# Splitting the token stage of batches 0 and 1: residual and second normalization moved into the next attention stage, with a new work order

## The chip, the core and the metric

The kernel runs on one core of a Trainium2 chip. A core has a matrix engine (PE, TensorE), a vector engine (DVE, VectorE), an activation engine (ACT, ScalarE), a general engine (POOL, GpSimd) and queues that issue DMAs (mostly SP's, some POOL's and ACT's). Each engine works through its own list of instructions in the order in which the program wrote them, and waits on semaphores for what it needs. The metric is the device time of one execution in microseconds (us); lower is better.

## The reference, cut to what matters

The input `x` is four images of 64 x 64 positions with 256 channels, float32. Two layers follow each other, and the batches do not depend on each other.

Layer 0 is self-attention over the 4096 positions of an image, with a residual:

```
f, g, v = xt @ Wf + bf, xt @ Wg + bg, xt @ Wh + bh
beta = softmax(einsum('bqd,bkd->bqk', g, f));  o = einsum('bqk,bkd->bqd', beta, v) @ Wo + bo
x = x + o
```

Layer 1 is a triangle attention over the 64 x 64 grid, and then a token block with two layer normalizations:

```
scores = einsum('bilhd,bljhd->biljh', q, k) / sqrt(d_k);  att = softmax(scores, axis=2)
out = einsum('biljh,bilhd,bljhd->bijhd', att, v1, v2)
h = layer_norm(x_in + out @ Wo, ln_agg_g, ln_agg_b)              # first norm
z = relu(h @ W1 + b1) @ W2 + b2 + h                              # MLP and residual
result = layer_norm(z, ln_out_g, ln_out_b)                       # second norm
```

The change concerns the last two lines of the token block (the residual `+ h` and the second norm) for batches 0 and 1, and the order in which the triangle's work of batches 1 and 2 is written out.

## The kernel before, in words

**Stages.** For each batch `b` in turn the kernel does layer 0 (`layer0`, 64 groups) and then the triangle of layer 1 (32 steps). The token block of batch `b` is not done in its own stage. It runs inside the triangle stage of batch `b + 1` (`next_layer1`), so that PE has token matmuls to do while DVE and POOL make the triangle's products. Batch 3 has no later triangle, and its tokens are done alone at the end. So the triangle stage of batch 1 carries the tokens of batch 0, that of batch 2 those of batch 1, and that of batch 3 those of batch 2 (there `own` is true).

**An attention group** (`score`, `values`): PE makes four score matmuls, ACT takes their exponential into `e` (two buffers), PE multiplies it with the values (`o`, L571), and DVE adds it to `esum` (L578). Every eight groups a query block is closed on DVE: the partial sums (L581 to L588), a reciprocal (L600), the product `oT` (L602) and two reductions (L610). In the next group PE multiplies `oT` with the output weights (L623), DVE adds bias and residual (L624), and the six groups after it begin with a projection of that result (L638). One thing more hangs on these groups in the attention stages of batches 2 and 3: `rest.recall` brings back the tokens of batch `b - 2`, 16 tiles of 256 tokens, one every three groups, and `rest.finish` scales them by the last gain and bias on POOL (L1248, L1249) and stores them.

**A triangle step** makes eight products of 128 x 2048 (L999): five or six on DVE (`R`, three buffers), three or two on POOL (`Rp`, two buffers). PE accumulates each product with eight short matmuls (L1009), ACT copies the result out (L1019), and SP stores it.

**A token tile** of 256 tokens goes through these words: `h0 h1` the output projection plus residual in PSUM (`hp`, L1081 and L1086), `sa` its mean and variance (L1097, L1098), `rr` and `pp` the inverse root (ACT, then seven tiny instructions on POOL), `fa` the first norm (`h`, L1158), `ht` its transpose on PE (L1181), `hT` and `hU` two scaled copies of the transpose (L1186; `hU` makes the one for the residual, with gain and both biases), `m0 m1 r0 r1` the hidden layer (L1214, L1223), `z0 z1` the second matmuls (L1234) followed by four transposes that add the residual in PSUM (`zp<-ident,hT`, L1240), `so` the sums of the second norm on ACT (L1112, L1116), `fo` its affine step (L1158), and `fi`, which for batches 0 and 1 stores the normalized tile to DRAM (`put_off`).

**The order** of all of this is a text, `ORDER`: 70 words, repeated once per period, 20 periods. A period holds two triangle steps and one token tile. `A13/1` is "step 2i + 1, accumulate product 3, one period late"; `/2` is two periods late. The words of one engine run in the order of the text. The scores of the later pairs (`sp`, L897) are in 11 of the periods. POOL also issues the DMAs that load the next batch's factors (`spread`) during steps 24 to 29.

Of the kernel before, what the change touches and what calls it, by code (L numbers as in the profile page):

```python
# [10 lines left out]
F32 = mybir.dt.float32  # L11
# [4 lines left out]
ALU = mybir.AluOpType  # L16
AX = mybir.AxisListType

P = 128
C = 256  # L20
# [9 lines left out]
NP = T // 256  # L30
# [10 lines left out]


ORDER = """
    r0/1 A10/2 A11/2 m1/1 R14/2 R05/1 S1/1 R15/2 T10/2 sp/1 A14/2 A16/2 r1/1 e0/1 e1/1 A15/2 A05/1 T11/2 R04/1
    A04/1 z0/1 W1/1 R03/1 V1/1 fi/2 S0 z1/1 t1/1 so/1 R06/1 R00/1 c1/1 sa A03/1 R07/1 R02/1 A06/1 A02/1 A00/1
    rr/1 pp/1 W0 R01/1 A07/1 A01/1 fo/1 fa T01/1 R12/1 t0 T00/1 R17/1 h1/-1 sf/1 R13/1 h0/-1 f0/1 ht f1/1 R16/1
# [20 lines left out]
def attention_then_triangle_kernel(  # L67
# [6 lines left out]
    nc = tc.nc  # L74
    NB = x.shape[0]
# [5 lines left out]
    work = ctx.enter_context(tc.tile_pool(name="work", bufs=2))  # L81
# [29 lines left out]
    back_t = ctile([P, 4], "back")  # L111
# [50 lines left out]
    lag_bc = brow(lag, C, "lag_bc")  # L162
# [327 lines left out]
    def layer0(b, F, safe, rest, ahead):  # L490
# [238 lines left out]
        for g in range(8 * NQB):  # L729
            qb, k = divmod(g, 8)  # L730
            if b == 0 and not safe:
                for load in later[3 * g : 3 * g + 3]:
                    load()
                if g == 6:
                    fold_bias()
                if g == 20:
                    add_b2()
            if safe and k == 0 and qb + 1 < NQB:
                mx, todo = pieces(qb + 1)
                for qc, t in todo:  # L740
                    max_piece(qc, t, mx)
                row[qb + 1] = max_row(mx)
            values(g, g + 1 < 8 * NQB)

            if qb > 0 and not (qb == last and k >= 6 + late):
                for part in parts[k]:
                    part(qb - 1)
            if late and g % 2 == 0 and 0 <= g // 2 - 2 < ahead.n:
                ahead.bring(g // 2 - 2)
            if late and g % 2 == 1 and 0 <= g // 2 - 3 < ahead.n:  # L750
                ahead.turn(g // 2 - 3)
            if b > 1 and g % 3 == 0 and g < 3 * NP:
                rest.recall(NP * (b - 2) + g // 3)
            if b > 1 and g % 3 == 2 and g < 3 * NP:
                rest.finish(NP * (b - 2) + g // 3)
            if qb == last and k == 3:
                L.fetch_v1(0)
                L.fetch_v1(1)
            if qb == last and k == 5:
                if b > 0:  # L760
                    rest.load(NP * (b - 1))
                L.fetch_qk(0, True)
# [49 lines left out]
        if old:  # L812
            rest.turn(t0)
            rest.load(t0 + 1)
            rest.normed(t0)
            rest.carried(t0)
        if not late:
            values1(1)
        score(2)
# [216 lines left out]
    class Tokens:  # L1036
        def __init__(self):
            self.ios = []
            self.A, self.htp = {}, {}
            self.h, self.hT, self.hT2, self.hid, self.z, self.zp, self.hps = {}, {}, {}, {}, {}, {}, {}  # L1040
            self.mv = self.rs = None
            self.raw = {}


        def put_off(self, tt):
            b, t = divmod(tt, NP)
            if t == 0:
                self.raw[b] = dram.tile([NP, P, 2, C], F32, tag="raw", name="raw")
            nc.sync.dma_start(out=self.raw[b][t], in_=self.z.pop(tt))

        def recall(self, tt):
            b, t = divmod(tt, NP)
            self.z[tt] = work.tile([P, 2, C], F32, tag="s4", name="z")
            nc.sync.dma_start(out=self.z[tt], in_=self.raw[b][t])

        def load(self, tt, far=False):
            b, t = divmod(tt, NP)
# [332 lines left out]
    def words_of(order):  # L1390
        for w in order:
            w, late = (w.split("/") + ["0"])[:2]
            yield w, int(late)
# [58 lines left out]
    def next_layer1(b, L, rest, ahead, F):  # L1452
        own = b == NB - 1
        t0 = NP * (b - 1)


        n2, n1, n0 = NP, NP + own, NP + 2 * own
        stored, held = set(), []
        mv, rs, rn, mps = {}, {}, {}, {}

        def fetched(step):
            if F is not None and 24 <= step < 31:
                ahead.fetch(F, b + 1, step)


        def load(q, far=False):
            if q < NP or 24 + (q - NP) // 2 in stored:
                rest.load(t0 + q, far)
            else:
                held.append((q, far))  # L1470

        def was_stored(step):
            stored.add(step)
            if own and step == 26:
                held.extend((NP + q, True) for q in (2, 3, 4))
            todo, held[:] = list(held), []
            for q, far in todo:
                load(q, far)

        def moments(q):  # L1480
            if q not in mv:
                mv[q] = small.tile([P, 4, 2], F32, tag="mv", name="mv")
            rest.mv = mv[q]

        def of_piece(word, q):
            tt = t0 + q
            first, second = 1 <= q < n1, 0 <= q < n2
            if word in ("h0", "h1"):
                if 2 <= q < n0:
                    n = int(word[1])  # L1490
                    rest.heads(tt, n, new=q not in mps)
                    mps.setdefault(q, {})["h", n] = True
                    if len(mps[q]) == 2 and q + 1 < n0:
                        load(q + 1)
            elif word == "sa" and first:
                moments(q - 1)
                rest.stats(rest.hps[t0 + q], 0)
            elif word == "so" and second:
                moments(q)
                z = rest.z[t0 + q] = work.tile([P, 2, C], F32, tag="s4", name="z")  # L1500
                rest.sums_of(rest.zp[t0 + q], z, rest.mv, 2)
            elif word == "rr" and second:
                moments(q)
                rest.roots(0 if q + 1 < n1 else 2, 4)
                rs[q] = rest.rs
            elif word == "pp" and second:
                moments(q)
                rest.rs = rs.pop(q)
                rest.polish(0 if q + 1 < n1 else 2, 4, nc.gpsimd, back=back_t)
                rn[q] = rest.rn  # L1510
            elif word == "fa" and first:
                rest.rn = rn[q - 1]
                rest.affine_a(tt)
            elif word == "fo" and second:
                rest.rn = rn[q]
                rest.affine_o(tt)
            elif word == "ht" and first:
                rest.turn(tt)
            elif word == "hT" and first:
                rest.normed(tt)  # L1520
            elif word == "hU" and first:
                rest.carried(tt)
            elif word in ("m0", "m1") and first:
                n = int(word[1])
                mps[q][n] = [rest.hidden(tt, fc) for fc in (2 * n, 2 * n + 1)]
            elif word in ("r0", "r1") and first:
                n = int(word[1])
                for fc, mp in zip((2 * n, 2 * n + 1), mps[q][n]):
                    rest.rectify(tt, fc, mp)
            elif word in ("z0", "z1") and second:  # L1530
                n = int(word[1])
                rest.outputs(tt, n, new=tt not in rest.zp)
                mps.setdefault(q, {})["z", n] = True
            elif word == "fi" and second:
                (rest.finish if own else rest.put_off)(tt)

        def spread(step):
            if F is not None:
                ahead.spread(F, b + 1, step)

        step_word, scores, take_scores = step_words(L, fetched, was_stored, spread)
        mps[1] = {}
        for period in range(NP + 4):
            for word, late in words_of(ORDER):
                i = period - late
                if i == 0 and word in ("A05", "A04"):
                    for m in (4, 5) if word == "A04" else ():
                        step_word("A", 0, m)
                elif word[0] in "RATSWVtc":
                    step_word(word[0], 2 * i + int(word[1]), int(word[-1]))  # L1550
                elif word in ("sp", "sf"):
                    if (i == 0) == (word == "sf"):
                        scores(i)
                elif word in ("e0", "e1", "f0", "f1"):
                    if (i == 0) == (word[0] == "f"):
                        take_scores(i, int(word[1]))
                else:
                    of_piece(word, i)
        assert not held
        if F is not None:  # L1560
            ahead.fetch(F, b + 1, NSTEP)
# [68 lines left out]
```

## Time and profile before

| | |
|---|---|
| median of 3 runs | 3651.67 us (3650.98 to 3653.79) |
| profiled execution, its own time | 3654.27 us |
| span of that execution, first to last instruction | 3652.5 us |
| busy in the span: PE, DVE, ACT, POOL | 97%, 75%, 53%, 49% |

The stages can be read off the timeline. The two that carry the changed words are the triangle stages of batch 1 (1303 to 1744 us) and of batch 2 (2175 to 2617 us). The two that receive the moved work are the attention stages of batches 2 and 3, which begin where those end and last about 396 us each up to the first instructions of the next triangle stage. A time of one instruction in the profile is longer than the distance to the next one on the same engine where they overlap, so the working below takes distances between starts where it can.

### The profile page before, as it was taken

The page shows a single profiled execution, that of the slowest core. Times are in us where ns is not written, and L with a number is a line of the kernel's source. Part 1 is how long each engine was busy: PE and PEld are TensorE (multiplying, and loading weights), DVE is VectorE, ACT ScalarE, POOL GpSimd, SP SyncE. Part 2 cuts the span into 40 slices and gives each one's busy share as a digit, 9 for nine tenths or more (in the row PEclk, how much of TensorE's full clock was granted, in tenths as well). Part 3 has the DMA queues.
Part 4 walks back from the last instruction along what each step waited for, and adds up shares of the span by engine and source line. Part 5 has one row for each costly group of instructions (what it writes and reads, how often), then busy time and mean ns, then how long its engine had stood idle before and what let it go on. Part 6 is the DMA issues. An engine that isn't in the chain of part 4 may idle for free.

```text
span 3652.5 us, 58549 instructions
## 1 busy us (share of the span) xinstructions
PE 3544.0 (97%) x22410; PEld 1909.6 (52%) x22410; DVE 2739.5 (75%) x2326; ACT 1934.8 (53%) x4209; POOL 1805.7 (49%) x918
## 2 busy tenths in 40 slices
PE   9999899988999999999999999999999999999998
PEld 6555444434555555554455555554455555555477
DVE  4777599996555479999565549999755556999976
ACT  3444455544444367666444457676544436777654
POOL 5000199994000068889311028889722106999910
PEclk9999999999999999999999999999999999999999
DMA  9544555465111343425422153333522225341221
GB/s 174 140 130 121 137 150 143 118 135 126 52 49 52 97 116 95 94 51 104 101 80 79 58 144 92 78 89 66 129 73 78 75 83 137 91 96 47 68 69 52
DMA packets 487987, 353.38 MB, mean 97 GB/s; under 512 B 302673, under 2 KB 433489, under 8 KB 478865
## 3 DMA queue, kind: packets, MB, share of 16 engines
q1 hardware_dynamic: 438656, 322.58, 33.1%
q0 software_dynamic: 36160, 19.94, 5.1%
q10 hardware_dynamic: 12880, 7.01, 0.7%
q8 instruction: 179, 2.93, 0.3%
q14 instruction: 112, 0.91, 0.1%
HBM read 197.34 MB, written 152.04 MB: 96 GB/s over the span
## 4 chain that ended last, share of the span: by engine, by line
PE 68%; POOL 5%; DVE 4%; issue 3%; ACT 2%; DMA 1%; SPq 0%; ACTq 0%; DVEq 0%; POOLq 0%
PE o L571 18%; PE acc L1009 15%; PE proj L638 6%; PE mp L1214 6%; PE zp L1234 5%; PE s L544 5%; POOL Rp L999 4%; DVE R L999 3%; PE sp L897 3%; PE hp L1081 3%; PE v1p L670 2%; PE y L623 1%; PE att L951 1%; PE htp L1181 1%; PE hp L1086 1%
## 5 line engine op out<-in xcount | busy, mean ns | idle before, releaser
L999 POOL TENSOR_TENSOR Rp<-attP,v 128x2048 f32<-128x2048 f32 x328 | 1491.1, 4576 | 463.3 <-ACT attP L959 367.8
L999 DVE TENSOR_TENSOR R<-att,v 128x2048 f32<-128x2048 f32 x696 | 1547.7, 2274 | 67.7 <-PE acc L1009 49.4
L571 PE MATMUL o<-e,v 128*128 128x512 f32 x2048 | 1043.6, 592 | 0.0
L578 DVE TENSOR_TENSOR esum<-esum,e 128x2048 f32<-128x2048 f32 x224 | 525.0, 2344 | 508.9 <-ACT e L556 505.6
L556 ACT ACTIVATE e<-s 128x1024 f32<-128x1024 f32 x512 | 523.4, 1024 | 581.3 <-PE s L544 484.6
L544 PE MATMUL s<-gT,fT 128*128 128x512 f32 x1024 | 785.6, 769 | 8.6 <-ACT e L556 5.1
L1009 PE MATMUL acc<-R,wsel 128*32 128x512 f32 x5568 | 705.7, 602 | 37.2 <-DVE R L999 29.4
L571 PEld LDWEIGHTS o<-e,v 128*128 128x128 f32 x2048 | 388.7, 190 | 275.9 <-issue 233.6
L1009 PE MATMUL acc<-Rp,wsel 128*32 128x512 f32 x2624 | 344.3, 596 | 11.1 <-POOL Rp L999 10.4
L1019 ACT COPY ao<-acc 128x1024 f32<-128x1024 f32 x256 | 254.4, 1021 | 189.6 <-PE acc L1009 153.1
L1009 PEld LDWEIGHTS acc<-R,wsel 128*32 128x32 f32 x5568 | 152.1, 109 | 384.5 <-issue 277.9
L544 PEld LDWEIGHTS s<-gT,fT 128*128 128x128 f32 x1024 | 194.2, 190 | 243.9 <-issue 231.0
L1142 POOL TENSOR_SCALAR nt<-mv 128x4 f32<-128x4 f32 (+1 forms) x51 | 9.8, 192 | 627.2 <-DVE mv L1098 623.1
L1248 POOL TENSOR_TENSOR z<-z,log_bc 128x512 f32<-128x512 f32 x48 | 71.8, 1496 | 452.2 <-DMA z<-raw 434.5
L934 ACT ACTIVATE es<-S,rd 128x64 f32<-128x64 f32 x1024 | 257.8, 336 | 16.6 <-DVE rd L926 13.8
L1214 PE MATMUL mp<-hT,w 128*128 128x256 f32 x1024 | 249.5, 389 | 0.7 <-ACT hT L1186 0.7
L1234 PE MATMUL zp<-w,hid 128*128 128x256 f32 x1024 | 245.0, 385 | 0.8 <-ACT hid L1223 0.8
L1214 PEld LDWEIGHTS mp<-hT,w 128*128 128x128 f32 x1024 | 186.8, 190 | 101.2 <-ACT attP L959 36.0
L1234 PEld LDWEIGHTS zp<-w,hid 128*128 128x128 f32 x1024 | 185.7, 190 | 62.3 <-issue 29.3
L600 DVE RECIPROCAL rec<-den 128x512 f32<-128x512 f32 x32 | 107.4, 3358 | 119.4 <-PE den L596 114.0
L1009 PEld LDWEIGHTS acc<-Rp,wsel 128*32 128x32 f32 x2624 | 81.5, 110 | 197.8 <-issue 139.0
L1223 ACT ACTIVATE hid<-mp,b_sb 128x256 f32<-128x256 f32 x256 | 105.2, 469 | 117.7 <-PE mp L1214 117.7
(180 smaller groups left out, 3665.7 us busy)
## 6 DMA issues: line engine op xcount, KB each, us to landing
v<-v2d SPq DMA_DIRECT2D x44, 512.0 KB
v1c<-v1d SPq DMA_DIRECT2D x128, 128.0 KB
aT<-ao SPq DMA_DIRECT2D x1024, 16.0 KB
A<-aT SPq DMA_DIRECT2D x256, 64.0 KB
out_dram<-z SPq DMA_DIRECT2D x63, 256.0 KB
y<-yT SPq DMA_DIRECT2D x56, 256.0 KB
q<-st SPq DMA_DIRECT2D x56, 256.0 KB
k<-st SPq DMA_DIRECT2D x52, 256.0 KB
```

The source lines that it names most:

```text
L544: nc.tensor.matmul(s_ps[r // 2][:, r % 2, :], fT[tt][:, ts(r * 4 + n, P)], gT[qb // 4][:, ts(qb % 4, QB)], start=True, stop=not safe,)
L556: nc.scalar.activation(e[g][:, 2 * j : 2 * j + 2, :], s_ps[j], AF.Exp)
L571: nc.tensor.matmul(o_ps[qb], F.v[tt][:, r * 4 + n, :], es[:, r, :], start=(k == 0 and r == 0), stop=(k == 7 and r == 3),)
L578: nc.vector.tensor_tensor(esum[qb], esum[qb], es, ALU.add)
L638: nc.tensor.matmul(ps, w[:, cc, rows], y(qb, cc), start=(cc == 0), stop=(cc == 1))
L897: nc.tensor.matmul(sp[ts(h, 64), lh, n, :], k[rows, u * 8 + n, :], q[rows, u * 8 + n, :], start=True, stop=True,)
L934: nc.scalar.mul(e[:, i, :], rows[:, i, :], rec[:, i : i + 1])
L999: eng.tensor_tensor(R, src.unsqueeze(1).to_broadcast([P, D, N]), v2[h], ALU.mult)
L1009: nc.tensor.matmul(acc[32 * c : 32 * c + 32, n % 2, :], w[:, n, c, 16 * h : 16 * h + 32], R[:, ts(c, 8), :].rearrange("p d j -> p (d j)"), ...
L1019: nc.scalar.copy(self.ao[step][:, ts(np, 2)].rearrange("p k d j -> p k (d j)"), self.acc[step][np])
L1214: nc.tensor.matmul(self.mp[:, fc % 2, :], w1_sb[:, cc, ts(fc, P)], self.hT[tt][:, cc, :], start=(cc == 0), stop=(cc == 1),)
L1234: nc.tensor.matmul(zp[:, n, :], self.hid[tt][:, fc, ts(n, P)], w2_sb[:, fc, :], start=(fc == 0), stop=(fc == 3 and tt not in self.hT2),)
```

## The change

In the triangle stages of batches 1 and 2 (`own` false) the token block now ends at the MLP. `hU` no longer makes a scaled copy of the transpose; it stores the normalized `h` to DRAM (`carried_off`). With no `hT2`, the outputs have no transposes after them. `so` is one copy of `zp` to SBUF, and `fi` stores that (`summed_off`). `fo` falls away, and the inverse root (`rr`, `pp`) covers the first norm alone. The sums of the first norm (`sa`) move from DVE to ACT. DRAM tile `raw` holds both parts.

In the attention stages of batches 2 and 3 each tile is brought back with both parts (`recall`, 512 KB in a buffer of tag `R`), and the rest is spread over the groups that follow, one engine per group: three groups later DVE adds residual and sum and takes the statistics (`settle`), then ACT the root (`rooted`), DVE its Newton step (`polished`), ACT the affine step (`scaled`), and POOL and SP the end (`finish`).

Batches 1 and 2 get a new `ORDER`; batch 3 keeps the old text as `ORDER_LAST`.

```diff
+ORDER = """
+    R03/2 R06/2 t1/2 h0 m0/1 R04/2 c1/2 A03/2 A07/2 R16/2 A04/2 A06/2 R12/2 R10/2 T00/2 fi/2 W0/1 sf/2 R17/2
+    T01/2 A10/2 A12/2 t0/1 R11/2 r0/1 fo/2 R13/2 R15/2 f1/2 h1 m1/1 f0/2 A11/2 c0/1 A16/2 V0/1 R14/2 r1/1 A13/2
+    A15/2 R00/1 A17/2 T10/2 A14/2 sp/1 R02/1 sa R05/1 e0/1 R01/1 z0/1 rr/1 T11/2 z1/1 pp/1 e1/1 so/1 A00/1 A05/1
+    R07/1 W1/1 A02/1 A01/1 fa S1 ht V1/1 S0 hU hT
+""".split()
-ORDER = """
+ORDER_LAST = """
     r0/1 A10/2 A11/2 m1/1 R14/2 R05/1 S1/1 R15/2 T10/2 sp/1 A14/2 A16/2 r1/1 e0/1 e1/1 A15/2 A05/1 T11/2 R04/1
     A04/1 z0/1 W1/1 R03/1 V1/1 fi/2 S0 z1/1 t1/1 so/1 R06/1 R00/1 c1/1 sa A03/1 R07/1 R02/1 A06/1 A02/1 A00/1
     rr/1 pp/1 W0 R01/1 A07/1 A01/1 fo/1 fa T01/1 R12/1 t0 T00/1 R17/1 h1/-1 sf/1 R13/1 h0/-1 f0/1 ht f1/1 R16/1
     hU A13/1 hT A12/1 A17/1 R11/1 c0 R10/1 m0 V0
...
-            if b > 1 and g % 3 == 0 and g < 3 * NP:
-                rest.recall(NP * (b - 2) + g // 3)
-            if b > 1 and g % 3 == 2 and g < 3 * NP:
-                rest.finish(NP * (b - 2) + g // 3)
+            if b > 1:
+                for do, late in ((rest.finish, 7), (rest.scaled, 6), (rest.polished, 5), (rest.rooted, 4), (rest.settle, 3), (rest.recall, 0)):
+                    if (g - late) % 3 == 0 and 0 <= g - late < 3 * NP:
+                        do(NP * (b - 2) + (g - late) // 3)
...
+        def carried_off(self, tt):
+            self.put_off(tt, 0, self.h.pop(tt))
+
+        def summed_off(self, tt):
+            self.put_off(tt, 1, self.z.pop(tt))
...
+            self.both[tt] = work.tile([P, 2, 2, C], F32, tag="R", name="hz", bufs=3)
+            nc.sync.dma_start(out=self.both[tt], in_=self.raw[b][t])
+
+        def settle(self, tt):
+            both = self.both.pop(tt)
+            h, z = both[:, 0], both[:, 1]
+            nc.vector.tensor_tensor(h, h, lag_bc.unsqueeze(1).to_broadcast([P, 2, C]), ALU.mult)
+            nc.vector.tensor_tensor(h, h, lb2_bc.unsqueeze(1).to_broadcast([P, 2, C]), ALU.add)
+            nc.vector.tensor_tensor(z, z, h, ALU.add)
+            self.z[tt] = z
+            self.stats(z, 2)
...
             elif word == "sa" and first:
                 moments(q - 1)
-                rest.stats(rest.hps[t0 + q], 0)
+                if own:
+                    rest.stats(rest.hps[tt], 0)
+                else:
+                    junk = work.tile([P, 2, C], F32, tag="sx", name="junk", bufs=1)
+                    rest.sums_of(rest.hps[tt], junk, rest.mv, 0)
             elif word == "so" and second:
...
+                if own:
+                    moments(q)
+                    rest.sums_of(rest.zp[tt], z, rest.mv, 2)
+                else:
+                    nc.scalar.copy(z, rest.zp.pop(tt))
+            elif word == "rr" and second and (own or q + 1 < n1):
...
-            for word, late in words_of(ORDER):
+            for word, late in words_of(ORDER_LAST if own else ORDER):
```

More of the change, by code (lines that the diff above doesn't have):

```diff
@@ L815, in layer0 @@
             rest.normed(t0)
-            rest.carried(t0)
+            (rest.carried if b == NB - 1 else rest.carried_off)(t0)
         if not late:
@@ L1041, in __init__, with put_off, rooted, polished @@
             self.mv = self.rs = None
-            self.raw = {}
-        def put_off(self, tt):
+            self.raw, self.both, self.settled = {}, {}, {}
+        def put_off(self, tt, part, src):
             b, t = divmod(tt, NP)
-            if t == 0:
-                self.raw[b] = dram.tile([NP, P, 2, C], F32, tag="raw", name="raw")
-            nc.sync.dma_start(out=self.raw[b][t], in_=self.z.pop(tt))
+            if b not in self.raw:
+                self.raw[b] = dram.tile([NP, P, 2, 2, C], F32, tag="raw", name="raw")
+            nc.sync.dma_start(out=self.raw[b][t][:, part], in_=src)
+        def carried_off(self, tt):
+            self.put_off(tt, 0, self.h.pop(tt))
+        def summed_off(self, tt):
+            self.put_off(tt, 1, self.z.pop(tt))
         def recall(self, tt):
             b, t = divmod(tt, NP)
-            self.z[tt] = work.tile([P, 2, C], F32, tag="s4", name="z")
-            nc.sync.dma_start(out=self.z[tt], in_=self.raw[b][t])
+            self.both[tt] = work.tile([P, 2, 2, C], F32, tag="R", name="hz", bufs=3)
[8 more added lines that the diff above has]
+            self.stats(z, 2)
+            self.settled[tt] = self.mv
+            self.mv = None
+        def rooted(self, tt):
+            self.mv = self.settled.pop(tt)
+            self.roots(2, 4)
+            self.settled[tt], self.mv = (self.mv, self.rs), None
+        def polished(self, tt):
+            self.mv, self.rs = self.settled.pop(tt)
+            self.polish(2, 4, nc.vector)
+            self.settled[tt] = self.rn
+        def scaled(self, tt):
+            self.rn = self.settled.pop(tt)
+            self.affine(self.z[tt], self.z[tt], 2)
         def load(self, tt, far=False):
@@ L1496, in of_piece @@
                 moments(q - 1)
-                rest.stats(rest.hps[t0 + q], 0)
-            elif word == "so" and second:
-                moments(q)
[L1500 to L1504, printed above, removed]
+                if own:
[3 more added lines that the diff above has]
+                    rest.sums_of(rest.hps[tt], junk, rest.mv, 0)
+            elif word == "so" and second:
+                z = rest.z[tt] = work.tile([P, 2, C], F32, tag="s4", name="z")
+                if own:
[4 more added lines that the diff above has]
+            elif word == "rr" and second and (own or q + 1 < n1):
+                moments(q)
+                rest.roots(0 if q + 1 < n1 else 2, 4 if own else 2)
                 rs[q] = rest.rs
-            elif word == "pp" and second:
+            elif word == "pp" and second and (own or q + 1 < n1):
                 moments(q)
                 rest.rs = rs.pop(q)
-                rest.polish(0 if q + 1 < n1 else 2, 4, nc.gpsimd, back=back_t)
+                if own:
+                    rest.polish(0 if q + 1 < n1 else 2, 4, nc.gpsimd, back=back_t)
+                else:
+                    rest.polish(0, 2, nc.gpsimd, back=back_t[:, 2:4])
                 rn[q] = rest.rn
@@ L1513, in of_piece @@
                 rest.affine_a(tt)
-            elif word == "fo" and second:
+            elif word == "fo" and second and own:
                 rest.rn = rn[q]
@@ L1521, in of_piece @@
             elif word == "hU" and first:
-                rest.carried(tt)
+                (rest.carried if own else rest.carried_off)(tt)
             elif word in ("m0", "m1") and first:
@@ L1534, in of_piece @@
             elif word == "fi" and second:
-                (rest.finish if own else rest.put_off)(tt)
+                (rest.finish if own else rest.summed_off)(tt)
         def spread(step):
@@ L1543, in next_layer1 @@
         for period in range(NP + 4):
-            for word, late in words_of(ORDER):
+            for word, late in words_of(ORDER_LAST if own else ORDER):
                 i = period - late
-                if i == 0 and word in ("A05", "A04"):
+                if own and i == 0 and word in ("A05", "A04"):
                     for m in (4, 5) if word == "A04" else ():
```

## The prediction

> **What bounds the kernel now.** I read the busy row, then the table of stretches (columns: PE, PE's weight loads, DVE, ACT, POOL busy, each with a count; granted clock, DMA share, GB/s), cut where the stages change.
>
> ```profile
> PE 3544.0 (97%) x22410; PEld 1909.6 (52%) x22410; DVE 2739.5 (75%) x2326; ACT 1934.8 (53%) x4209; POOL 1805.7 (49%) x918
> ...
> 1303.30:1636.10 332.80, 331.43 (x3001) 178.68 (x3000) 318.72 (x227) 232.62 (x642) 289.54 (x145) 1.00 0.37 87
> 1636.10:1731.00 94.90, 90.97 (x657) 43.32 (x660) 92.62 (x64) 59.71 (x182) 91.39 (x57) 1.00 0.58 105
> 1731.00:1744.40 13.40, 8.72 (x77) 1.98 (x69) 12.31 (x6) 3.85 (x5) 11.71 (x7) 1.00 0.20 36
> 1744.40:2140.00 395.60, 392.60 (x1104) 207.33 (x1100) 220.10 (x137) 163.51 (x183) 62.16 (x33) 1.00 0.29 84
> ```
>
> The triangle stage of batch 1 has two regimes. Up to 1636 us PE is never idle (1.4 us in 333). After it there are no scores `sp` left, PE has 1.9 us less per period, and POOL, which now also issues factor DMAs, is 96% busy. The attention stage that receives the moved work is PE's: 392.6 of 395.6 us, DVE at 56%.
>
> The PE timeline of one period (start, us, instruction) gives prices:
>
> ```profile
> 1448.14 1.99 PE L1234 MATMUL zp<-w,hid 128*128 128x256 f32 x8
> 1449.97 0.38 PE L1240 MATMUL zp<-ident,hT 128*128 128x128 f32 x2
> 1450.19 1.89 PE L1234 MATMUL zp<-w,hid 128*128 128x256 f32 x8
> 1451.91 0.38 PE L1240 MATMUL zp<-ident,hT 128*128 128x128 f32 x2
> 1452.13 0.60 PE L951 MATMUL att<-ident,es 128*128 128x128 f32 x4
> ```
>
> From start to start two residual transposes hold PE 0.22 us, so 0.44 us per tile. The period is 27.76 us (an `att` at 1430.19 and again at 1457.95).
>
> In the attention stage what matters is how late DVE may be once per query block. Its timeline around a block's end, then the projection that waits for it:
>
> ```profile
> 1889.38 3.36 DVE L600 RECIPROCAL rec<-den 128x512 f32<-128x512 f32 x1 [3.75 <-PE den L596]
> ...
> 1894.57 2.28 DVE L578 TENSOR_TENSOR esum<-esum,e 128x2048 f32<-128x2048 f32 x1
> 1896.77 1.40 DVE L624 SCALAR_TENSOR_TENSOR yT<-y,bo_sb,yT 128x512 f32<-128x512 f32 x2
> ...
> 1899.71 0.59 PE L638 MATMUL proj<-yT,wq 128*128 128x512 f32 x1
> ```
>
> L624 ends at 1898.17, PE needs it at 1899.71: 1.54 us of slack.
>
> **What the Trainium skill says.** "TensorE: Matmul & The Clock Gate", Part 4: PE-mode transpose, gives about 275 ns for a 128 x 128 transpose inside a kernel. The row here has 273 ns, but only 0.11 us from one to the next, and that distance is what PE gets back. "Perfetto Trace Analysis", Optimization Strategy, warns that the most-contended engine can change with the regime; the table above shows it, PE then POOL. "SBUF — State Buffer", SBUF: two separate sides, says that a DVE operation with two SBUF inputs and a POOL operation lock each other out. The trace agrees: an `esum` add takes 3.24 us instead of 2.29 when POOL's 1.27 us scaling starts with it at 1876.8, so I allow about 1 us where moved DVE work meets `finish`.
>
> **The change, part by part** (own time 3654.27 us, 2.6 above the median of the runs).
>
> *PE, first regime.* Per stage 64 transposes (4 x 16 tiles) go: 64 x 0.11 = 7.0 us. Twelve of the sixteen tiles lie in the PE-bound stretch: 12 x 0.44 = 5.3 us. Runs of accumulations also cost 0.12 us at their end (five take 4.43 us, 1443.71 to 1448.14, where 5 x 0.862 is 4.31). The old order has four such runs per period, the new one three (A03 to A12, A11 to A14, A00 to A01): 12 x 0.12 = 1.4 us.
>
> *Can the others keep up with 27.76 - 0.56 = 27.2 us?* DVE has 11 products x 2.21 (five in 11.07) + 2 x 0.84 for sums = 26.0; its statistics (1.16 us) have moved away. POOL has 5 x 4.55 + 1.7 = 24.5. ACT loses `fo` (0.91) and `hU` (0.90), keeps one set of sums (1.76) where it was, and gains one copy of 0.5. All fit, but three chains are near the limit. (1) `z1` to `ht` to `m0`. From the end of the `z1` matmuls: 0.26 until ACT starts (1452.13 to 1452.39), copy 0.49, eight `es` of W1 1.93, then the two halves of `fa`, the last ending 1.02 later: 3.70. PE has A00, A05, A02, A01 in between, 4 x 0.862 + 0.12 = 3.57, and the first transpose needs only the first half: 0.08 us lost. Then V1 (0.97) and `hT` end at 5.58; PE reaches `m0` at 5.71. (2) A10 needs R10, whose buffer A03 frees: 1.13 us (1443.71 to 1444.84) + 2.29 = 3.42 after A03 starts; PE gets there after 4 x 0.862 = 3.45. (3) A05 needs `e1`, about 0.8 us to spare. So I charge 0.08 x 12 = 1.0 us. First regime: 5.3 + 1.4 - 1.0 = 5.7 us gained.
>
> *POOL, last regime.* From R06 of step 24 on POOL has 19 products and six DMA pairs in both orders, 102 us almost without a gap, and neither PE (25.3 us per period) nor DVE (26.0) matters against its 27.1. It loses one of four root polishes (1.7 us), since the last tile has no second norm. In the old order DVE finishes the stage 4.1 us after POOL's last product (1740.3 to 1744.4). In the new one the last products of DVE and POOL end together: with `z1` of the last tile, DVE has eight products left (17.7 us after A00, 0.9), POOL four (18.2). Two accumulations, 1.8 us, follow: 2.3 us gained. Sum 4.0 us.
>
> So about 9.7 us per stage; I take 9.2 for small waits between buffers. Two stages: 18.4 us.
>
> *Attention stages.* Per tile DVE gets three 128x512 operations (0.66 each), two statistics (1.09) and four tiny ones (0.16 each): 3.1 + 0.6 us. 16 tiles x 3.7 = 59 us on a DVE that idles 175 us. ACT gets two tiny ones and 0.91 us, in gaps of about 1.1. PE gets nothing. Cover: DVE idles about 2 us per 4.35 us group, and `e` has two buffers. In the attention stage of batch 0 DVE already does eight transposes (2.0 us) in every odd group, and PE is 100% busy from 100 to 400 us. The cover is missing where a `settle` stands right before the L624 of a block. It falls in groups 3, 6, ... 48; groups 24 and 48 are the first of a block, after the L610 reductions and before `esum` and L624. There L624 is 3.1 us later with 1.54 us of slack: PE loses about 1.6 us at the projection. In a block's last group (15, 39) it delays a copy that had 3.75 us of idleness after it; in its second (9, 33) it comes after L624. Two such places per stage, two stages: 4 x 1.6 = 6.4 us lost. Bounds: 0 if PE's wait can be taken elsewhere, 13 if settles near a block's end cost as much too.
>
> *DMA.* Write and read of a second 256 KB per tile. The store of `h` holds the only buffer of tag `h` until the next period's `fa`, some 25 us. The load has three groups, over 13 us. SP's list per period keeps its length plus one issue. Priced at 0; behind it the first `settle`, whose load queues after the 3 MB for the next batch: 0 to 2 us, once per stage.
>
> Sum: 3654.3 - 18.4 + 6.4 = 3642.3 of its own time, less 2.6: **3639.5 us**, -0.33%.
>
> **Rivals.**
> (a) *Attention stages take it all for nothing.* The batch 0 stage speaks for it (2 us per odd group, no loss). Then 3651.7 - 18.4 = 3633.
> (b) *The chain over `so`, W1, `fa`, `hT` becomes a wait.* It has nothing to spare; 0.5 us more in each of 12 periods in two stages takes 12 us back: 3651.5. What speaks against it is that all of its terms are distances read from this trace.
> (c) *Slower: DVE's extra 3.7 us stall PE at every tile.* DVE is in order; an exponential of group g + 2 waits for the `esum` add of g, with 2 to 3 us of slack in a group without projection (one add ends at 1763.70, and the exponential into its buffer starts after 1765.76, when the next group's `e` is complete), and POOL's lock adds 1 us. PE would lose at 32 tiles. Against the stages' 18.4 us it decides from 0.6 us per tile on; at 1 us it gives 3665. Against it: only 6 us of bursts fall together in any two groups outside the block's end, and 4 us of idleness lie in them.
> (d) *The change doesn't do what it says,* because PE is not the bound but DVE, at 96% in the first regime. But DVE is relieved by 1.16 us per period, more than PE; only if its buffers hold it does the gain shrink, to the 8 us of the last regime, and with the 6.4 lost it would be no change.
>
> **How the numbers follow.** The likeliest sum 0.54, (a) 0.12, (b) and (d) together 0.20, (c) 0.14. A difference under 0.2%, 7.3 us, is about what a measurement of this kernel cannot tell from none. The likeliest case's own range is 3633 to 3646; some of it lies above 3644.4. Faster: 0.48 + 0.12 = 0.60; same: 0.06 + 0.18 = 0.24; slower: 0.02 + 0.14 = 0.16. The range takes (a), down to 3630, and (b), up to 3657; it leaves out (c).
>
> **What would show it.** Right: no `zp<-ident` rows in the two stages; a period of about 27.2 us; PE's idle before `htp` and `mp` under 0.2 us a period; each stage some 9 us shorter; PE waiting 1 to 2 us for L624 at the first projection of two blocks in each receiving stage, and nowhere else there. Wrong: waits of PE for ACT's `h` or `hT` in every period (b); an attention stage longer by more than 8 us, with PE waiting for `e` (c); a period still near 27.8 us with PE idle for `R` (d).

## The result and the profile after

| | before | after |
|---|---|---|
| median | 3652.73 us (4 runs, 3650.98 to 3655.10) | 3631.03 us (4 runs, 3628.52 to 3633.54) |
| profiled execution, its own time | 3654.27 us | 3633.17 us |
| span of that execution | 3652.5 us | 3631.4 us |

The ratio is 0.994, with a 95% interval from 0.9928 to 0.9953. The predicted time was 3639.5 us. The direction held; the gain is 21.7 us between the medians where about 12 were worked out. The time lies only 1 us inside the lower end of the range that the prediction gave (3630 to 3657 us).

To see where it came from I cut both traces at the same two events in batches 1 and 2. A triangle stage runs from the end of the last residual transpose of its first token tile (the second `hp<-ident`) to the first score of the next attention stage; an attention stage runs from there to its last `den<-esum`.

| stage | before | after | difference | predicted |
|---|---|---|---|---|
| triangle of batch 1 | 441.18 | 428.46 | -12.7 | -9.2 |
| attention of batch 2 | 391.22 | 394.38 | +3.2 | +3.2 |
| triangle of batch 2 | 441.28 | 428.46 | -12.8 | -9.2 |
| attention of batch 3 | 391.16 | 394.44 | +3.3 | +3.2 |

These add up to -19.1 us. The last stage has the old order and the old length: its last vector instruction ends 19.3 us earlier than before (3645.33 against 3626.06). From there to the end of the span it was 7.1 us before and 5.3 after; these 1.8 us lie after the last computation, where the final store lands. No edit touches that part and the eleven traces of the experiments have 5.2 to 5.9 us there, so what they are stays open.

The table of stretches of the kernel after, cut where the regimes change (columns as before: PE, PE's weight loads, DVE, ACT, POOL busy with counts; granted clock, DMA share, GB/s):

```profile
1303.00:1629.80 326.80, 326.80 (x2985) 175.48 (x2984) 312.37 (x181) 217.52 (x622) 290.62 (x146) 1.00 0.41 100
1629.80:1731.40 101.60, 93.67 (x682) 41.99 (x680) 98.25 (x55) 53.70 (x155) 99.33 (x55) 0.98 0.58 103
1731.40:2126.00 394.60, 389.37 (x1087) 204.19 (x1084) 272.35 (x312) 184.63 (x247) 52.41 (x34) 1.00 0.31 93
```

The two regimes are still there. In the first PE is busy for the whole stretch; in the second POOL is at 98%. In the attention stage DVE went from 220 to 272 us, 52 us more, and PE shows 5 us of idleness instead of 3.

**First regime.** The PE timeline after, at two successive transposes of `h`, gives the new period:

```profile
1583.10 0.66 PE L1220 MATMUL htp<-ident,h 128*128 128x128 f32 x4
...
1610.21 0.66 PE L1220 MATMUL htp<-ident,h 128*128 128x128 f32 x4
```

27.11 us, where it was 27.76: 0.65 us per period and not 0.48. There are no `zp<-ident` rows in between.

**Second regime.** The POOL timeline before, at the start of the stretch in which POOL is the bound and at its last products:

```profile
1638.22 4.58 POOL L999 TENSOR_TENSOR Rp<-attP,v 128x2048 f32<-128x2048 f32 x1 [1.19 <-issue]
...
1731.21 9.08 POOL L999 TENSOR_TENSOR Rp<-attP,v 128x2048 f32<-128x2048 f32 x2
```

The POOL timeline after shows its last products and the factor DMAs behind them:

```profile
1706.86 22.66 POOL L1007 TENSOR_TENSOR Rp<-attP,v 128x2048 f32<-128x2048 f32 x5
1729.81 1.32 POOL L274 DMA_DIRECT2D fT<-ahgf  x2 [0.30 <-POOL Rp L1007]
```

From the end of POOL's product 5 of step 24 to the end of its last one it took 103.2 us before (1637.05 to 1740.29) and 99.7 after (1629.79 to 1729.52). From the last product to the first score it took 4.1 us before and 1.9 after (1731.42).

**Attention stage.** PE's waits after, in the stage of batch 2 (line waited for: us in total, times, longest):

```profile
PE proj L646 <- DVE yT L632: 1.9, 2, 1.0
PE s L552 <- ACT e L564: 1.3, 2, 1.1
PE den L606 <- DVE esum L591: 1.2, 1, 1.2
PE s L552 <- ACT ao L1027: 0.5, 1, 0.5
PE y L631 <- DVE oT L610: 0.3, 1, 0.3
```

The first and the last row are new; the other three had the same figures before. The DVE timeline after, at group 24, shows the cause, and the PE timeline its end (L632 and L646 are the L624 and L638 of the kernel before):

```profile
1881.87 0.68 DVE L618 TENSOR_REDUCE dens<-esum 128x1 f32<-128x512 f32 x1
1882.46 0.68 DVE L1073 TENSOR_TENSOR hz<-hz,lag_bc 128x512 f32<-128x512 f32 x1
...
1885.72 2.26 DVE L586 TENSOR_TENSOR esum<-esum,e 128x2048 f32<-128x2048 f32 x1
1887.89 1.40 DVE L632 SCALAR_TENSOR_TENSOR yT<-y,bo_sb,yT 128x512 f32<-128x512 f32 x2
```

```profile
1888.69 0.70 PE L646 MATMUL proj<-yT,wq 128*128 128x512 f32 x1 [0.93 <-DVE yT L632]
```

`settle` stands from 1882.46 to 1885.72 between the reductions and the add, and the projection waits 0.93 us for what comes behind it.

### The profile page after: what moved, and what is told of

Read it like the earlier page. It is cut to its first block, busy times and chain, and to the rows that moved or that the text cites. A ratio compares the mean times of both kernels' runs of the same rounds, so it can differ in the third digit from the quotient of the medians.

```text
span 3631.4 us, 58644 instructions
## 1 busy us (share of the span) xinstructions
PE 3522.3 (97%) x22282; PEld 1895.3 (52%) x22282; DVE 2823.5 (78%) x2558; ACT 1923.8 (53%) x4221; POOL 1779.2 (49%) x904
## 4 chain that ended last, share of the span: by engine, by line
PE 67%; POOL 8%; DVE 6%; issue 4%; ACT 1%; DMA 1%; SPq 0%; ACTq 0%; POOLq 0%; DVEq 0%
PE o L579 16%; PE acc L1017 16%; POOL Rp L1007 7%; PE proj L646 6%; PE mp L1253 5%; PE zp L1273 5%; PE s L552 4%; PE sp L905 3%; PE hp L1120 3%; DVE R L1007 2%; PE v1p L678 2%; PE att L959 1%; PE y L631 1%; DVE rec L608 1%; PE htp L1220 1%
## 5 line engine op out<-in xcount | busy, mean ns | idle before, releaser
L1287 POOL TENSOR_TENSOR hz<-hz,log_bc 128x512 f32<-128x512 f32 x32 | 47.1, 1471 | 542.8 <-ACT hz L1197 474.4
L1181 POOL TENSOR_SCALAR nt<-mv 128x2 f32<-128x2 f32 (+1 forms) x49 | 9.4, 192 | 565.2 <-DVE mv L1137 560.1
L915 ACT ACTIVATE S<-sp 128x512 f32<-128x512 f32 x128 | 131.6, 1094 | 78.0 <-PE sp L905 78.0
```

## The experiments

Each is an edit of the changed kernel. Theory A is the prediction's account: PE bounds the first regime, POOL the second, and the attention stage pays only where a `settle` stands ahead of a late L632.

### The settle ahead of the block's parts

```diff
+            if b > 1 and k == 0 and g % 3 == 0 and 0 < g <= 3 * NP:
+                rest.settle(NP * (b - 2) + g // 3 - 1)
             if qb > 0 and not (qb == last and k >= 6 + late):
                 for part in parts[k]:
                     part(qb - 1)
...
-                    if (g - late) % 3 == 0 and 0 <= g - late < 3 * NP:
+                    if (g - late) % 3 == 0 and 0 <= g - late < 3 * NP and not (late == 3 and k == 0):
```

> In groups 24 and 48 of an attention stage, settle stands ahead of the block's reciprocal instead of behind its reductions; nothing else changes. Theory A (the attention stages' loss comes from settle standing before L632 in a block's first group, 1.2 us at each of two places in the trace of after): the two attention stages, from the first scores to the last den, shrink from 394.4 us by 2.4 us each to 392.0, the wait of PE for yT at the projection goes, and the time falls by about 5 us to 3626. Rival B (DVE has simply more to do in these stages, wherever it stands): both stages stay at 394.4 and the time at 3631.

Measured: 3625.82 us (ratio 0.9931, 0.9915 to 0.9948). Triangle stages 428.46 and 428.45, unchanged; attention stages 392.05 and 392.00, 2.4 us shorter each. PE's waits in the attention stage of batch 2:

```profile
PE s L552 <- ACT e L564: 1.3, 2, 1.1
PE den L606 <- DVE esum L591: 1.2, 1, 1.2
PE s L552 <- ACT ao L1029: 0.5, 1, 0.5
PE y L631 <- DVE oT L610: 0.3, 1, 0.3
```

The row for `yT` is gone, the others stay. So 2.4 of the 3.2 us are the settles of groups 24 and 48, shown by moving them. The 0.8 left lies at the end of the first block, where the offset of its output matmul `y` (L623 before, L631 after) from the stage's start is 47.55 us before and 48.34 after. In the DVE timeline after, the `settle` of group 6 ends there just ahead of the block's last `esum` add, and the add itself stretches, to 3.33 us instead of 2.29, while POOL's `finish` of another tile runs:

```profile
1763.72 0.69 DVE L1073 TENSOR_TENSOR hz<-hz,lag_bc 128x512 f32<-128x512 f32 x1
...
1766.98 3.33 DVE L586 TENSOR_TENSOR esum<-esum,e 128x2048 f32<-128x2048 f32 x1
```

How the 0.8 us are shared between the two, no run separates.

### The old order with the new split

```diff
-            for word, late in words_of(ORDER_LAST if own else ORDER):
+            for word, late in words_of(ORDER_LAST):
...
-                if own and i == 0 and word in ("A05", "A04"):
+                if i == 0 and word in ("A05", "A04"):
```

> The split token stage with the old order of words for all three batches. Theory A (the transposes give 0.44 us per period where PE bounds, and the new order gives the rest by fewer ends of accumulation runs and a shorter end of the stage): period 27.3 us, triangle stages about 434 us against 441.2 before and 428.5 after, time about 3642. Rival C (the gain is the transposes' alone): 428.5 and 3631. Rival D (the gain is the order's alone): 441 and 3655.

Measured: 3643.80 us (0.9976, 0.9965 to 0.9987). Triangle stages 434.78 and 434.81, attention stages 394.37 and 394.34. The stage's 12.7 us split in halves: 6.4 from the work taken out, 6.3 from the order. The period is 27.32 us (`htp` at 1593.99 and 1621.31): 0.44 us less than before, the price of four transposes to the hundredth. The order is worth 0.21 us more per period. Most of the rest of its share is the end of the stage; the POOL timeline of this kernel shows it:

```profile
1709.64 22.65 POOL L1007 TENSOR_TENSOR Rp<-attP,v 128x2048 f32<-128x2048 f32 x5
1735.17 1.32 POOL L274 DMA_DIRECT2D fT<-ahgf  x2 [2.88 <-issue]
```

POOL's last product ends at 1732.29, 2.6 us later in the stage than after the change, and its next instruction stands 2.88 us behind it, where the changed order had 0.30. From that last product to the first score of the next stage it is 5.6 us (1732.29 to 1737.88), where the changed order has 1.9: these 3.7 us are the larger part of what the order gives.

### The residual transposes kept

Each half of `zp` gets two transposes of `hT` again, ahead of its matmuls. The first matmul starts the sum anew and writes over them, so they add only their time on PE.

```diff
+        rest.again = not own
...
+            if self.again and apart is None:
+                for cc in range(2):
+                    nc.tensor.transpose(zp[:, n, ts(cc, P)], self.hT[tt][:, cc, ts(n, P)], ident)
```

> The changed kernel, with four transposes of the hidden layer's input put ahead of z0 and z1 into the same PSUM tile, which the matmuls then overwrite: PE has its work back, nothing else. Theory A (PE bounds the first regime, POOL the last): the period goes from 27.1 to 27.55 us over 12 periods, each of the two triangle stages from 428.5 to 433.8, the time to 3642. Rival D (PE is not the bound, the gain came from DVE's relief and the order): 428.5 and 3631.

Measured: 3639.28 us (0.9967, 0.9955 to 0.998); triangle stages 433.72 and 433.23, 5.0 us more on average; attention stages unchanged. The period is 27.50 us, 0.39 more: from start to start the four transposes hold PE for 0.49 us, and the `zp` matmuls between them take 0.10 less than without them (3.55 for 3.65). PE's time is the bound of the first regime: what is put back on it comes back in every period.

### The first norm's sums on DVE again

```diff
-                if own:
-                    rest.stats(rest.hps[tt], 0)
-                else:
-                    junk = work.tile([P, 2, C], F32, tag="sx", name="junk", bufs=1)
-                    rest.sums_of(rest.hps[tt], junk, rest.mv, 0)
+                rest.stats(rest.hps[tt], 0)
...
-                    rest.polish(0, 2, nc.gpsimd, back=back_t[:, 2:4])
+                    rest.polish(0, 2, nc.gpsimd, back=back_t)
```

The second line only takes the constants that belong to DVE's form of the sums.

> The changed kernel with the first norm's statistics back on DVE in the two triangle stages. DVE then needs 27.15 us per period against 27.1 of PE and 27.1 of POOL's last regime. Theory A (PE bounds, DVE has 1.1 us to spare): stages 1 to 6 us longer each, 429.5 to 434, time 3633 to 3643. Rival D (DVE's relief made the gain): 8 us or more longer each, 436 to 441, time 3647 or more.

Measured: 3638.66 us (0.9963, 0.9951 to 0.9976); triangle stages 433.53 and 433.59, 5.1 us more. The period is 27.43 us, 0.32 more, although PE does nothing more and its busy row is full in both. Of the lost time 0.21 us are inside the row of the transposes, and the rest stands around the `mp` matmuls behind them. First the PE timeline of this kernel, then its ACT timeline:

```profile
1581.20 0.87 PE L1220 MATMUL htp<-ident,h 128*128 128x128 f32 x4
```

```profile
1575.79 0.30 ACT L1163 ACTIVATE ln<-mv,eps 128x2 f32<-128x2 f32 x1 [0.62 <-DVE mv L1137]
...
1580.45 1.02 ACT L1197 ACTIVATE h<-hp,rn 128x256 f32<-128x256 f32 x2
```

ACT waits 0.62 us for DVE's statistics and comes late to everything behind them. Its second half of `h` ends at 1581.47, after the transposes have begun at 1581.20, and they take 0.87 us instead of 0.66. In the changed kernel `h` ends at 1583.04 and the transposes begin at 1583.10. That is the chain of rival (b): it has about a tenth of a microsecond to spare, and this edit, which makes `h` a third of a microsecond later against the transposes, makes it a bound.

### The factor loads on SP's queue

For batches 2 and 3 the loads of `gT` and the lower half of `fT` in steps 24 to 29 are issued by SP instead of POOL (`spread_g` and `spread_f` get a queue, and for SP's they view the destination as plain float32).

```diff
-                    spread_g(F, step - 24, d, half)
+                    spread_g(F, step - 24, d, half, nc.sync if b > 1 else nc.gpsimd)
...
-                    spread_f(F, r, d, 0)
+                    spread_f(F, r, d, 0, nc.sync if b > 1 else nc.gpsimd)
```

> The changed kernel, with the loads of the next batch's factors during the triangle stages of batches 1 and 2 issued from SP's queue instead of POOL's. Theory A (POOL bounds the last regime, from step 24 on, and 8 us of its 100 us there are these issues): POOL's need falls to 24.4 us per period and DVE's 26.0 takes over; each of the two stages about 3 us shorter, 425.5, time about 3625. Rival E (the end of the stage hangs on DVE's and PE's products, POOL's issues fill gaps): 428.5 and 3631. Rival F (SP's queue is late and the next attention stage waits for its factors): 428.5 or more and a wait of PE for a DMA.

Measured: 3629.06 us (0.9936, 0.9919 to 0.9952), not told apart from the changed kernel. Yet the triangle stages fell to 425.90 and 425.86, 2.6 us each: POOL's issues were on the path. The attention stages rose to 397.04 and 395.34, and that needed a cause. ACT's waits in this kernel from 1728 to 1745 us:

```profile
ACT e L564 <- DMA aT<-ao: 4.8, 1, 4.8
```

and PE's, in the attention stage:

```profile
PE s L552 <- ACT e L564: 2.3, 2, 2.1
```

The exponentials `e` and the triangle's output `ao` take turns in the buffers of one tag (`k8`). The second `e` of the stage gets the buffer of the last `ao`, and that is held until its eight stores on SP have landed. In both kernels SP issues these stores at the same distance behind the first score (1.2 to 5.6 us), but here the exponential that waits for them starts 7.8 us behind it instead of 6.8, and PE waits 2.1 us instead of 1.1. Why they land later is not shown. This is about what the stage of batch 3 lost (0.9 us). That of batch 2 lost 1.7 us more, and the table of stretches, cut 5 us long just behind that wait in either stage, shows what those are (the last three columns are clock, DMA share, GB/s):

```profile
1737.39:1742.39 5.00, 5.00 (x10) 2.53 (x10) 2.29 (x1) 1.89 (x2) 0.00 (x0) 0.66 1.02 433
2600.18:2605.18 5.00, 5.00 (x14) 2.76 (x15) 2.44 (x2) 2.91 (x3) 0.00 (x0) 1.00 1.02 434
```

At 0.66 of the clock, 5 us of work lose 1.7.

### Both edits, and the changed kernel once more

> Both edits in one kernel: settle ahead of the reciprocal in a block's first group, and the factor loads from SP's queue. Theory A: the two gains add, about 5 and 6 us, time about 3620. Rival: only the first one counts, 3626.

Measured: 3626.34 us (0.9926, 0.991 to 0.9943). Triangle stages 425.89 and 425.88; attention stages 393.02 and 394.66, now with the slow stretch in the second. Of the 5.1 us that the triangles gain over the settle alone the attention stages give 3.6 back, as before, and the total is not told apart from that of the settle alone (3625.82 us).

> The changed kernel again, unedited, beside the two others on the same chip: 3631, triangle stages 428.5, attention stages 394.4, the same under every theory.

Measured: 3629.24 us (0.9942, 0.9925 to 0.9959), stages 428.87, 394.37, 428.73, 394.34. The stages of the changed kernel repeat within 0.5 us; the differences of the edits above, 1 to 6 us per stage, are larger.

### Half of the last step's stores on POOL's queue

```diff
-                nc.sync.dma_start(
+                queue = nc.gpsimd if step == NSTEP - 1 and d % 2 else nc.sync
+                queue.dma_start(
```

> With the settle first and the factor loads on SP, and in addition half of the eight stores of a stage's last triangle step issued by POOL instead of SP. Theory (the 1.0 us per attention stage that the factor loads on SP cost is one wait: the exponential of the second group takes the buffer of the last step's ao, which its eight stores on SP's queue hold, 4.8 us of ACT idle and 2.1 us of PE at the stage's start): with four stores per queue the wait falls by more than 2 us, PE's 2.1 us go, the attention stages take about 391 us each, and the second stage's further 1.7 us (a stretch at a lower clock just after that wait) may go with it. 3626.3 less 4 to 6: about 3621. Rival (the loss comes from the loads themselves, or POOL's issue is too slow): 392 to 394 us as now, 3626.

> With the settle first, factor loads on POOL as in the changed kernel, and half of the eight stores of a stage's last triangle step issued by POOL instead of SP. Theory: the 1.1 us that PE waits for the exponential of the second group at the start of each attention stage is the same wait for ao's stores, so it goes: 391 us per stage instead of 392.05, about 3623. Rival (that wait has another cause): 392.05 and 3625.8.

Measured: 3642.46 us (0.9977, 0.9967 to 0.9986) and 3648.66 us (0.9991, 0.9983 to 1.0): 16 and 23 us worse than without the split. Triangle stages are unchanged (425.89 and 428.55); the attention stages take 401.79 and 400.99 us in the first and 402.33 and 401.77 in the second. Both expectations failed. PE's waits in the first kernel's attention stage of batch 2, and then POOL's timeline at the start of that stage:

```profile
PE s L552 <- ACT e L564: 3.9, 2, 3.7
PE s L552 <- DMA fT<-ahgf: 3.6, 1, 3.6
```

```profile
1730.15 2.98 POOL L1039 DMA_DIRECT2D aT<-ao  x4 [6.02 <-ACT ao L1029]
1733.12 2.62 POOL L274 DMA_DIRECT2D fT<-ahgf  x4
```

POOL worked through its list in order. Its four loads of the upper half of `fT`, issued at 1725.62 in the kernel without the split, now stand behind a wait for the last `ao` and behind four stores, and are issued at 1733.12. PE waits 3.6 us for them. The buffer comes free no sooner: POOL has issued its four stores by 1733.1, but the last of them lands only at 1737.8, and the exponential that needs the buffer starts at 1738.0, against 1736.1 without the split. After either wait the clock is at 0.66 for 5 us. The sum for the first stage, against 392.03 with the settle alone: 2.6 more for `e` (3.7 less 1.1), 3.6 for `fT`, two slow stretches of 1.7: 9.6 of the 9.8 measured. So these two runs say nothing against the buffer as the cause, but do not show it either.

### The last `ao` in a buffer of its own

The last step's `ao` goes to a buffer of tag R, of the same size and idle at that point. No DMA moves.

```diff
+                if step == NSTEP - 1 and self.b < 3:
+                    self.ao[step] = work.tile([P, 4, 8, N], F32, tag="R", name="ao", bufs=3)
+                else:
+                    self.ao[step] = work.tile([P, 4, 8, N], F32, tag="k8", name="ao")
```

> With the settle first and the factor loads on SP, all eight stores of a stage's last triangle step on SP as in the changed kernel, but the ao of that step (batches 0 to 2) in a buffer of tag R, so that no exponential takes a buffer that those stores hold; no DMA changes its queue or place. Theory (the 2.1 us of PE at the start of an attention stage is the wait for that buffer alone): ACT's wait for the stores and PE's 2.1 us go, the attention stages of batches 2 and 3 take about 391 us each, and the total is 4 to 7 us under the 3626.3 of the kernel with both edits: 3620 to 3622. Rival (the loads that follow the stores are late as well): the wait only moves to a score or a value matmul that needs the upper half of the factors, and the time stays at 3624 to 3627.

> With the settle first, factor loads on POOL as in the changed kernel, and the last step's ao (batches 0 to 2) in a buffer of tag R. Theory: PE's 1.1 us before the scores of the second group go, attention stages of 391 us, about 3 us under the 3625.8 of the settle first alone: 3622 to 3624. Rival (that wait is not for the buffer): 392.05 us per stage and 3625.8.

Measured: 3619.25 us (0.991, 0.9896 to 0.9924) with both edits, 3624.00 us (0.9924, 0.9909 to 0.9938) with the settle alone. The totals are 7.1 and 1.8 us under those of the same kernels without this edit. The second difference is no larger than the spread of the runs; the stages show it clearly. All four attention stages take 390.54 to 390.56 us, 0.6 less than before the change, where PE had the first 1.1 us of this wait too. ACT's waits of the first from 1715 to 1745 us, where the row with the DMA is gone:

```profile
ACT ao L1032 <- PE acc L1019: 12.3, 3, 7.7
ACT e L564 <- PE s L552: 6.5, 6, 1.2
```

So the buffer was the cause. The kernel with all three edits (settle first, factor loads on SP, a buffer of its own for the last `ao`) is the fastest here, about 12 us under the changed kernel and 32 under the kernel before.

## Why the prediction was right, and where it was off

The direction and the two bounds were right. That the time fell inside the range is in part luck: its lower end had been drawn for rival (a), which did not happen, the likeliest case's own range (3633 to 3646 us) was missed, and the changed kernel run again gave 3629.24 us, just below the range. (The prediction's last subtraction is also 0.2 us off: 3642.3 less 2.6 is 3639.7.)

**PE bounds the first regime: right.** The transposes returned what their distance of 0.11 us says: 0.44 us per period in the kernel with the old order, 0.39 when they were put back. The period was to be 27.2 and is 27.11.

**Run ends (12 x 0.12 us): the size came, but not from there.** The order gives 0.21 us per period. The new order has three runs for four, as the sum said, but the accumulations of a period with their run ends take 14.28 us before and after. What shrank are rows behind them: the two `mp` groups from 3.84 to 3.66 us, now behind `hp` and no longer behind accumulations, and the two `att` groups from 1.02 to 0.92. The `zp` matmuls took 0.09 more.

**The charge of 0.08 us per period for chain (1): not paid.** `h` ends 0.06 us ahead of the transposes where the sum had it 0.13 behind (3.70 against 3.57). That it is near the limit was right; the run with the statistics on DVE shows what happens beyond it. Up to POOL's product 5 of step 24 the stage gained 7.0 us, against 5.7 in the sum.

**POOL's last regime: the mechanism right, one term forecast at half its size.** The end gave 2.2 us against 2.3. The stretch before it gave 3.5 against the 1.7 of one root polish. Two things were mis-sized. The 102 us that the prediction counted begin at 1638.22; just ahead of them the order before has an idle gap of 1.19 us, the new order has none there, and the sum had left it out. And a root polish, priced at 1.7 us, costs POOL 1.98 from product to product where it follows a product, as all four did before (1644.12 to 1650.65, less one product of 4.55), and 1.82 where it follows a pair of issues, as the three do now (1631.21 to 1633.03): 2.5 us less. Together that is 3.7 by the distances and 3.5 measured. Why POOL was idle in the gap the profile does not show. That POOL's issues are on this path is shown by the run that moves them: 2.6 us per stage.

**The 9.2 us per stage** are thus 12.7: 1.3 more in the first regime, 1.8 more in POOL's, and no allowance of 0.5 for waits between buffers, which did not come.

**Attention stages, 2 x 1.6 us each: the total right by luck, the places partly.** The two places named cost 1.2 us each, because the slack of 1.54 us was read too small: it runs from the end of both halves of L624 to the first projection, and that one needs the first half alone. The second halves in the kernel before, on DVE and on PE:

```profile
1897.43 0.74 DVE L624 SCALAR_TENSOR_TENSOR yT<-y,bo_sb,yT 128x512 f32<-128x512 f32 x1
```

```profile
1900.14 0.59 PE L638 MATMUL proj<-yT,wq 128*128 128x512 f32 x1
```

The first half ends at about 1897.5 and is needed at 1899.71, the second ends at 1898.17 and is needed at 1900.14: 2.2 and 2.0 us of slack against the 3.26 that `settle` lasts. The other 0.8 are at the first block's end, which the bounds had mentioned and the sum had set to nothing. That the two errors cancel is chance.

**The first settle's load, 0 to 2 us: 0.** No wait of PE leads back to it.

**Rivals.** (a) fell: the stage does pay, and the run with the settle first shows for what. (b) did not happen in the changed kernel, but is about 0.1 us away. (c) fell: apart from the stage's first groups PE never waits for an exponential. (d) fell with the transposes that cost PE their time again when they were put back.

## What to carry to other kernels

Price work removed from a saturated in-order engine by the distance to the next instruction, and read the slack of the chains beside it from the same timeline; here a tenth of a microsecond separated two bounds. When moved work falls in a place where a consumer is due, put it ahead of the wait that has idle time anyway: calling `settle` a few instructions earlier was worth 2.4 us per stage. A stage's first allocations can wait for the stores of the stage before it, so follow what releases them: here a buffer shared with a store cost PE 1.1 to 2.1 us per stage. And a DMA moved to another queue also delays all that this queue was to issue next.

## What the runs showed of the hardware

The granted clock can fall after short waits of PE. In eight of the profiles (before, after, and six of the edits), from 1300 to 3480 us, PE has 28 waits of 2.1 to 4.5 us; in the 5 us behind them the clock is 0.50 to 0.74 in 18 cases, mostly 0.66, and full in 10. Behind the 46 waits of 1.1 to 1.8 us it is never below full. In all thirteen profiles the clock records have 24 such stretches there, each at half clock, 22 of them 3.41 us long and two 6.83. The same wait, 2.11 us at the same place of two stages, is followed by 0.66 in one and 1.00 in the other. The Trainium skill, "TensorE: Matmul & The Clock Gate", Part 1: The HAM clock gate, says that the clock halves after an idle window of about 3.4 us and returns after a busy one, and that the windows run freely. The length of the slow stretches agrees, at 3.41 us (half speed for that long in 5 us is the mean of 0.66), and free windows would make it a matter of chance. But the waits ahead of them here are as short as 2.1 us. Such a wait costs its own length and, when PE is the bound, 1.7 us more for each 3.41 us at half clock. Where PE is not the bound it cost nothing here: of the changed kernel's two triangle stages the first has a slow stretch in POOL's regime, the second has none, and both take 428.46 us.
